# Another order of all steps, and batch 28 turned on VectorE, in a conditional adapter kernel

## The chip, the cores and the metric

One core of one Trainium2 chip. The engines are TensorE (PE in the profile, its weight loads PEld), VectorE (DVE), ScalarE (ACT), GpSimd (POOL) and SyncE (SP), which here only issues DMAs. The metric is the device time of one execution in microseconds; the median of several executions is given.

## The reference

For each of 128 batches, x is 128 x 512 in float32, and an index from 0 to 9 (cut to the range) picks the weights of one of ten languages. The batch goes down to 128 columns, through relu, up to 512 again, is added to x, normalized over its 512 columns, scaled and shifted, and added to x once more.

```python
w1 = W1[language_ids]
w2 = W2[language_ids]
h = jnp.einsum('bsh,bha->bsa', hidden_states, w1) + b1[language_ids][:, None, :]
h = jax.nn.relu(h)
adapted = jnp.einsum('bsa,bah->bsh', h, w2) + b2[language_ids][:, None, :]
x = hidden_states + adapted
mean = jnp.mean(x, axis=-1, keepdims=True)
var = jnp.mean(jnp.square(x - mean), axis=-1, keepdims=True)
normed = (x - mean) * jax.lax.rsqrt(var + LN_EPS)
return normed * gamma[language_ids][:, None, :] + beta[language_ids][:, None, :]
# and outside: x + that
```

## The kernel before

Every batch is one tile of 128 x 512. Its steps, with the engine of each, are: `transpose_x` (PE, four transposes into the one `pxT` buffer), `copy_xT` (ScalarE, to SBUF), `stage_w1` (a copy of the language's W1 into a `w1s` buffer, by ScalarE or, for batches of kind c, by GpSimd), `down` (PE, four matmuls into the one `ph` buffer), `relu` (ScalarE), `up` (PE, one matmul, shown as two, into one of five `py` buffers), `add_b2` (GpSimd, x + b2 into one of four `r` buffers), `residual` (VectorE, py + r with its row sum), `square` (ScalarE, with its row sum), then for a pair of batches `scalar_means` and `deviation` (ScalarE, the root) and three small steps `rstd` (VectorE), then `scale` (VectorE, by gamma), `add_beta` (GpSimd, x + beta into an output tile `o`, of which there are eight pairs) and `finish` (VectorE, which is the last to read `py`), and `store` of the pair (SyncE). x is loaded in pairs, x_g for batches 2g and 2g + 1, into eight buffers.

A string KINDS says where b2 comes in: P by `add_b2`, E by `seed` (ScalarE copies x into `py` first and `up` adds to it; `residual` then adds b2), D by an extra step `vector_b2` of VectorE, M by a small matmul. A string TURNS says how x is transposed and W1 arrives: T on PE with W1 staged by ScalarE, c the same with W1 staged by GpSimd, w with W1 loaded from memory, F "turned": W1 by four DMAs (`load_rows`), x by four more in blocks of 32 columns (`load_blocks`), and `turn_blocks`, one transpose on VectorE in place of four on PE and `copy_xT`.

The order is written out by hand. Each step has a place in batches in the table STEPS, its offset from its own batch: one tuple for the first 32 batches, one of 16 that repeats to batch 111, one for the last 16 batches. X_STEPS does the same for the loads of x from pair 10 on. All steps are sorted by batch + offset, and `keep` makes each engine run its own in that order. Of the last batches (E = 123) the steps stand in a written-out list, with `b2_of`, `beta_of`, `end_of`, `store_pair` and `store_last` for the same work. So a place decides nothing but the order on each engine's queue; each step still waits for its inputs and buffers. Each engine reads the language numbers of four batches at a time (`lid`).

Of the kernel before, what the change touches and what calls it, by code (L numbers as in the profile page):

```python
# [1008 lines left out]
```

## Time and profile before

| | |
|---|---|
| median of 3 runs | 301.0 us (300.9 to 301.27) |
| the profiled execution | 300.62 us, of which its span is 298.9 us |
| mean granted TensorE clock | 0.997 |
| busy: PE, DVE, ACT, POOL | 97%, 97%, 92%, 93% of the span |
| DMA | 85.22 MB, mean 285 GB/s |
| the chain that ended last | PE 75%, DMA 9%, POOL 6%, DVE 3% |

The span runs from the first to the last instruction of the profiled execution. In the profile L440 is `transpose_x`, L444 `copy_xT`, L431 `stage_w1`, L463 `down`, L471 `relu`, L477 and L485 `up`, L450 `add_b2`, L503 `residual`, L526 `square`, L569 `scale`, L457 `add_beta`, L578 `finish`, L663 `end_of`, L409 `turn_blocks`, L188 the load of an x pair, L397 and L403 the loads of a turned batch, L582 `store`, L695 and L698 the stores at the end. A line of waits gives the engine and line that waited, what it waited for, the total in us, how often, and the longest.

### The profile page before, as it was taken

To read this page: it belongs to the slowest core of one execution; us is meant where nothing else is said; L and a number is where in the kernel's file an instruction comes from. 1 tells how busy PE (TensorE), PEld (TensorE's weight loads), DVE (VectorE), ACT (ScalarE), POOL (GpSimd) and SP (SyncE) were. 2 spreads that over 40 slices of the span, in tenths; PEclk is the share of its full clock that TensorE was granted. 3 is DMA by queue.
4 is the path that set the end of the run, shared out by engine and by line. 5 is a ranking of instruction groups with operands and counts; after the bars stand their busy time and mean duration, and the time that the engine had idled before them with its cause. 6 is when DMAs were issued, how large, how long until landed. Compare 5 with 4: busy or idle time off the path is not lost.

```text
span 298.9 us, 7366 instructions
## 1 busy us (share of the span) xinstructions
PE 290.5 (97%) x1783; PEld 215.7 (72%) x1783; DVE 288.5 (97%) x775; ACT 274.4 (92%) x761; POOL 276.8 (93%) x239
## 2 busy tenths in 40 slices
PE   7899999999999999999999999999999999999993
PEld 3658777777776777767777777777777777777760
DVE  6989999999999999899999999999999999999996
ACT  5878789999999999989999999999999999899993
POOL 1299998999999999999899999999899999999992
PEclk9999999999999999999999999999999999999998
DMA  6999999955978798986999399986989879884907
GB/s 226 392 388 368 345 330 401 404 221 182 325 242 315 232 315 208 374 278 211 326 303 356 134 302 289 335 276 217 333 220 397 288 258 281 314 274 147 313 4 281
DMA packets 61100, 85.22 MB, mean 285 GB/s; under 512 B 4057, under 2 KB 25060, under 8 KB 61058
## 3 DMA queue, kind: packets, MB, share of 16 engines
q1 hardware_dynamic: 60998, 84.71, 84.1%
q8 instruction: 15, 0.25, 0.3%
q14 instruction: 27, 0.22, 0.2%
q10 hardware_dynamic: 60, 0.05, 0.1%
HBM read 51.19 MB, written 33.55 MB: 284 GB/s over the span
## 4 chain that ended last, share of the span: by engine, by line
PE 75%; DMA 9%; POOL 6%; DVE 3%; issue 3%; SPq 1%; POOLq 1%; ACT 1%; ACTq 0%; DVEq 0%
PE ph L463 30%; PE py L485 23%; PE pxT L440 14%; PE py L477 8%; POOL o L457 3%; DMA out_dram<-o 3%; DMA w<-in_L_cond_W_dram 3%; POOL r L450 2%; DMA x<-in_x_dram 2%; DVE py L503 1%; DVE o L663 1%; SPq L276 1%; POOLq L258 1%; DVE n L669 0%; DVE py L569 0%
## 5 line engine op out<-in xcount | busy, mean ns | idle before, releaser
L457 POOL TENSOR_TENSOR o<-x,beta_b 128x512 f32<-128x512 f32 x121 | 153.8, 1297 | 14.4 <-DVE beta_b L358 11.6
L463 PEld LDWEIGHTS ph<-xT,w1s 128*128 128x128 f32 x1024 | 126.8, 192 | 14.8 <-ACT hT L471 8.5
L463 PE MATMUL ph<-xT,w1s 128*128 128x128 f32 x1024 | 135.5, 275 | 0.3 <-DMA w1s<-in_L_cond_W_dram 0.2
L450 POOL TENSOR_TENSOR r<-x,b_b 128x512 f32<-128x512 f32 x83 | 107.1, 1299 | 1.6 <-DMA x<-in_x_dram 1.6
L485 PE MATMUL py<-w,hT 128*128 x196 | 101.1, 598 | 0.2 <-DMA w<-in_L_cond_W_dram 0.2
L440 PEld LDWEIGHTS pxT<-ident,x 128*128 128x128 f32 x468 | 59.9, 150 | 53.4 <-issue 39.9
L569 DVE SCALAR_TENSOR_TENSOR py<-py,nmean,gamma_b 128x512 f32<-128x512 f32 x124 | 93.1, 752 | 0.0
L578 DVE SCALAR_TENSOR_TENSOR o<-py,rstd,o 128x512 f32<-128x512 f32 x116 | 85.7, 746 | 2.7 <-DVE py L569 1.6
L526 ACT ACTIVATE sq<-py,sum 128x512 f32<-128x512 f32 x124 | 85.5, 690 | 0.4 <-DVE rstd L545 0.3
L444 ACT COPY xT<-pxT 128x512 f32<-128x512 f32 x117 | 68.6, 586 | 5.6 <-PE pxT L440 5.5
L440 PE MATMUL pxT<-ident,x 128*128 128x128 f32 x468 | 71.2, 275 | 1.3 <-ACT gamma_b L343 0.7
L503 DVE SCALAR_TENSOR_TENSOR py<-py,r 128x512 f32<-128x512 f32 x88 | 60.8, 691 | 0.7 <-PE py L485 0.5
L471 ACT ACTIVATE hT<-ph,b1T 128x128 f32<-128x128 f32 x128 | 47.3, 369 | 8.2 <-PE ph L463 5.9
L431 ACT COPY w1s<-w 128x512 f32 x80 | 48.6, 618 | 1.2 <-issue 1.2
L485 PEld LDWEIGHTS py<-w,hT 128*128 128x128 f32 x196 | 29.9, 192 | 2.4 <-DMA w<-in_L_cond_W_dram 0.7
L477 PE MATMUL py<-w,hT 128*128 x60 | 30.7, 594 | 0.0
L526 ACT ACTIVATION_READ_ACCUMULATOR sq<-py,sum 128x1 f32 x124 | 25.5, 205 | 0.0
L503 DVE SCALAR_TENSOR_TENSOR py<-py,b_b 128x512 f32<-128x512 f32 x30 | 20.6, 688 | 0.0
L423 ACT COPY py<-x 128x512 f32<-128x512 f32 x30 | 17.9, 598 | 0.2 <-DVE o L578 0.2
L536 ACT ACTIVATE root<-ssq,eps 128x2 f32<-128x2 f32 x62 | 16.8, 271 | 0.4
L517 ACT ACTIVATE nmean<-sum 128x2 f32<-128x2 f32 x61 | 12.6, 207 | 0.5 <-DVE py L503 0.2
L503 DVE DVE_READ_ACCUMULATOR py<-py,r 128x1 f32 x88 | 12.3, 140 | 0.0
(80 smaller groups left out, 149.4 us busy)
## 6 DMA issues: line engine op xcount, KB each, us to landing
x<-in_x_dram SPq DMA_DIRECT2D x64, 512.0 KB, 5.6
out_dram<-o SPq DMA_DIRECT2D x62, 512.0 KB, 4.5
w1s<-in_L_cond_W_dram SPq DMA_DIRECT2D x25, 256.0 KB, 7.4
w1s<-in_L_cond_W_dram SPq DMA_DIRECT2D x44, 64.0 KB, 4.9
x<-in_x_dram SPq DMA_DIRECT2D x44, 64.0 KB, 2.3
w<-in_L_cond_W_dram SPq DMA_DIRECT2D x4, 640.0 KB, 8.1
w<-in_L_cond_W_dram SPq DMA_DIRECT2D x1, 1792.0 KB, 9.8
w<-in_L_cond_W_dram SPq DMA_DIRECT2D x1, 768.0 KB, 5.3
```

The source lines that it names most:

```text
L431: keep(nc.gpsimd.tensor_copy(dst, src) if gpsimd else nc.scalar.copy(dst, src))
L440: keep(nc.tensor.transpose(pxs[b][:, k, :], cols, ident))
L444: keep(nc.scalar.copy(xT[b], pxs.pop(b)))
L450: keep(nc.gpsimd.tensor_tensor(rs[b], xb(b), b2_b[:, bass.ds(v * H, H)], ALU.add))
L457: keep(nc.gpsimd.tensor_tensor(os[g][:, j, :], xb(b), beta_b[:, bass.ds(v * H, H)], ALU.add))
L463: nc.tensor.matmul(phs[b], lhsT=w1s[b][:, k, :], rhs=xT_of(b, k), start=(k == 0), stop=(k == KC - 1))
L477: keep(nc.tensor.matmul(ys[b], lhsT=hT[b], rhs=cols, start=False, stop=True, skip_group_check=True))
L485: keep(nc.tensor.matmul(ys[b], lhsT=hT[b], rhs=w2[:, bass.ds(v * H, H)], start=not m, stop=True))
L503: nc.vector.scalar_tensor_tensor(ys[b], ys[b], 1.0, r, ALU.mult, ALU.add, accum_out=sum_of(b))
L526: nc.scalar.activation(sq, ys[b], AF.Square, bias=col(sums, b), scale=-float(H), accum_out=col(ssqs, b))
L569: nc.vector.scalar_tensor_tensor(ys[b], ys[b], col(nmeans, b), gamma_b[:, bass.ds(v * H, H)], ALU.add, ALU.mult)
L578: nc.vector.scalar_tensor_tensor(o, ys[b], rstds[g][:, j : j + 1], o, ALU.mult, ALU.add)
```

## The change

Batch 28 becomes a turned batch. Of the last 16 batches, 113 and 119 have W1 staged by ScalarE, 120 by GpSimd. Nearly all places in STEPS and X_STEPS change, those of the first 32 batches too, which had been the same from batch to batch; `up` of 2 and 3 come before `transpose_x` of 5. The loads of turned batches and of x and the stores stand at other places of SyncE's queue. The list of the end is in another order, with the stores of its pairs earlier in it. KINDS stays, and the work of every step stays as it was. The diff is cut to the tables that the text below speaks of and to both ends of the list.

```diff
@@ -22,122 +22,122 @@
-TURNS = ('TTTTTTTTTTTTTTTTTTTTTTTTTTTTTTTT', 'TTcTFTTTTTwTFTTT', 'ccccFcTcTcTTTTTT')
+TURNS = ('TTTTTTTTTTTTTTTTTTTTTTTTTTTTFTTT', 'TTcTFTTTTTwTFTTT', 'cTccFcTTccTTTTTT')
     "load": (
-        (0, 0, 0, 0, 0, 0, 0, 0, 0, 0, 0, 0, 0, 0, 0, 0, 0, 0, 0, 0, 0, 0, 0, 0, 0, 0, 0, 0, 0, 0, 0, 0,),
-        (0, 0, 0, 0, -4, 0, 0, 0, 0, 0, -2.81, 0, -3.51, 0, 0, 0,),
-        (0, 0, 0, 0, -6.42, 0, 0, 0, 0, 0, 0, 0, 0, 0, 0, 0,),
+        (0, 0, 0, 0, 0, 0, 0, 0, 0, 0, 0, 0, 0, 0, 0, 0, 0, 0, 0, 0, 0, 0, 0, 0, 0, 0, 0, 0, -0.68, 0, 0, 0,),
+        (0, 0, 0, 0, -4.44, 0, 0, 0, 0, 0, -0.85, 0, -5.67, 0, 0, 0,),
+        (0, 0, 0, 0, -1.63, 0, 0, 0, 0, 0, 0, 0, 0, 0, 0, 0,),
     "transpose": (
-        (0, 0, 0, 0, 0, 0, 0, 0, 0, 0, 0, 0, 0, 0, 0, 0, 0, 0, 0, 0, 0, 0, 0, 0, 0, 0, 0, 0, 0, 0, 0, 0,),
-        (-0.22, -0.2, -0.19, 0.29, 0, -1.03, -1.53, -0.9, -0.44, -0.96, -0.24, -0.56, 0, -1.37, -0.58, 0.02,),
-        (-0.56, -0.3, -0.31, -0.45, 0, -0.93, -0.02, -0.27, 0.56, 0.88, 0, 0, 0, 0, 0, 0,),
+        (-0.31, -0.37, -0.12, -0.15, -0.15, -1.1, -0.11, -0.19, -0.52, -0.01, -0.49, 0.07, -0.5, 0.09, -0.31, -0.17, 0.49, 0.48, 0.27, 0.16, -0.08, -0.14, -0.25, -0.24, -0.01, 0.08, -0.1, -0.4, 0, -1.6, -0.4, -0.11,),
+        (-0.55, -0.47, -0.47, -0.56, 0, -0.94, -0.75, -0.2, -0.56, -1.01, -0.6, -0.78, 0, -1.38, -0.09, -0.64,),
+        (-0.48, -0.29, -0.45, -0.66, 0, -1.11, -0.43, -0.17, 0.75, 1.66, 0, 0, 0, 0, 0, 0,),
     "turn": (
-        (0, 0, 0, 0, 0, 0, 0, 0, 0, 0, 0, 0, 0, 0, 0, 0, 0, 0, 0, 0, 0, 0, 0, 0, 0, 0, 0, 0, 0, 0, 0, 0,),
-        (0, 0, 0, 0, 0.2, 0, 0, 0, 0, 0, 0, 0, -0.57, 0, 0, 0,),
-        (0, 0, 0, 0, -0.45, 0, 0, 0, 0, 0, 0, 0, 0, 0, 0, 0,),
+        (0, 0, 0, 0, 0, 0, 0, 0, 0, 0, 0, 0, 0, 0, 0, 0, 0, 0, 0, 0, 0, 0, 0, 0, 0, 0, 0, 0, 0.09, 0, 0, 0,),
+        (0, 0, 0, 0, -0.49, 0, 0, 0, 0, 0, 0, 0, -0.22, 0, 0, 0,),
+        (0, 0, 0, 0, -0.31, 0, 0, 0, 0, 0, 0, 0, 0, 0, 0, 0,),
...
     "down": (
-        (1.1, 1.1, 1.1, 1.1, 1.1, 1.1, 1.1, 1.1, 1.1, 1.1, 1.1, 1.1, 1.1, 1.1, 1.1, 1.1, 1.1, 1.1, 1.1, 1.1, 1.1, 1.1, 1.1, 1.1, 1.1, 1.1, 1.1, 1.1, 1.1, 1.1, 1.1, 1.1,),
-        (1.07, 1.07, 1.42, 0.73, 0.41, 0.34, 0.33, 0.77, 0.9, 0.77, 0.77, 0.62, 0.63, 0.68, 1.17, 1.04,),
-        (1.28, 0.93, 0.89, 0.87, 1.38, 1.13, 1.04, 1.62, 3.44, 0, 0, 0, 0, 0, 0, 0,),
+        (0.58, 0.79, 1.2, 0.88, 1.31, 1.41, 1.09, 1.08, 1.09, 0.71, 1.29, 1.51, 1.26, 1.38, 1.03, 1.49, 1.6, 1.43, 1.17, 1.29, 1.22, 1.24, 1.21, 1.05, 1.34, 1.13, 0.85, 0.4, 1.03, 0.77, 0.96, 0.59,),
+        (1.04, 1.14, 0.56, 0.68, 0.15, 0.49, 0.89, 0.46, 0.06, 0.61, 1.09, 0.54, 1.06, 1.06, 0.9, 0.62,),
+        (1.27, 0.86, 0.57, 0.99, 1.01, 0.87, 2.29, 1.92, 3.7, 0, 0, 0, 0, 0, 0, 0,),
...
     "beta": (
-        (1.06, 1.06, 1.06, 1.06, 1.06, 1.06, 1.06, 1.06, 1.06, 1.06, 1.06, 1.06, 1.06, 1.06, 1.06, 1.06, 1.06, 1.06, 1.06, 1.06, 1.06, 1.06, 1.06, 1.06, 1.06, 1.06, -0.13, -0.13, -0.13, -0.13, -0.13, -0.13,),
-        (-1.6, 2.27, 3.38, 2.95, -2.25, -1, -1.17, 1.07, 3.14, 1.65, 4.45, 0.87, 4.05, -0.07, 3.92, 4.77,),
-        (-0.44, -0.9, 2.33, 3.63, 7.85, 8.64, 1.39, 1.88, 5.26, 0, 0, 0, 0, 0, 0, 0,),
+        (2.03, 2.01, 2.58, 2.49, 0.89, -1.02, 3.47, -0.14, 1.3, 0.42, 0.71, -0.16, -1.59, 5.06, 0.69, 3.45, 5.63, 3.93, 1.82, 4.4, 1.71, 3, 5.36, 2.46, 1.64, 2.84, -0.2, 3.34, 2.23, 1.46, 0.1, 4.86,),
+        (0.07, 3.23, 5.05, 2.81, 0.16, -2.13, 3.04, -1.64, 4.08, 4.47, 4.97, 1.01, 6.29, -1.87, 3.56, 4.55,),
+        (-1.83, 5.97, 4.7, 5.01, 5.92, 11.06, 1.95, -1.25, 4.58, 0, 0, 0, 0, 0, 0, 0,),
     "seed": (
-        (0, 0, 0, 0, 0, 0, 0, 0, 0, 0, 0, 0, 0, 0, 0, 0, 0, 0, 0, 0, 0, 0, 0, 0, 0, 0, 0, 0, 1.69, 0, 0, 0,),
-        (1.8, 0, 0, 0, 0, 0, 1.37, 0, 1.91, 0, 1.58, 0, 2.14, 0, 0, 0,),
-        (1.5, 0, 1.96, 0, 2.03, 0, 0, 0, 7.66, 0, 0, 0, 0, 0, 0, 0,),
+        (0, 0, 0, 0, 0, 0, 0, 0, 0, 0, 0, 0, 0, 0, 0, 0, 0, 0, 0, 0, 0, 0, 0, 0, 0, 0, 0, 0, 1.94, 0, 0, 0,),
+        (1.83, 0, 0, 0, 0, 0, 1.64, 0, 1.87, 0, 1.57, 0, 1.83, 0, 0, 0,),
+        (1.6, 0, 1.85, 0, 1.74, 0, 0, 0, 8.35, 0, 0, 0, 0, 0, 0, 0,),
     "up": (
-        (2.5, 2.5, 2.5, 2.5, 2.5, 2.5, 2.5, 2.5, 2.5, 2.5, 2.5, 2.5, 2.5, 2.5, 2.5, 2.5, 2.5, 2.5, 2.5, 2.5, 2.5, 2.5, 2.5, 2.5, 2.5, 2.5, 2.66, 2.66, 2.66, 2.66, 2.66, 2.66,),
-        (2.44, 2.68, 2.08, 2.03, 2.03, 1.39, 2, 2.68, 2.19, 2.18, 2.2, 2.11, 2.48, 2.43, 2.57, 2.35,),
-        (2.34, 2.49, 2.18, 2.48, 2.67, 2.21, 3.39, 8.45, 0, 0, 0, 0, 0, 0, 0, 0,),
+        (2.23, 2.32, 0.5, 0.32, 2.51, 2.23, 2.46, 2.37, 2.58, 2.39, 2.87, 2.33, 2.52, 2.22, 3.07, 2.75, 2.59, 2.31, 2.64, 2.54, 2.68, 2.47, 2.19, 2.87, 2.5, 2.11, 2.41, 2.74, 2.27, 1.97, 1.68, 2.12,),
+        (2.16, 2.67, 2.08, 1.36, 1.79, 2.32, 1.91, 1.84, 2.1, 2.52, 2.1, 2.22, 2.26, 2.18, 1.9, 2.37,),
+        (2.22, 2.73, 2.72, 2.49, 1.93, 3.53, 3.92, 7.16, 0, 0, 0, 0, 0, 0, 0, 0,),
...
     "end": (
-        (6.66, 6.66, 6.66, 6.66, 6.66, 6.66, 6.66, 6.66, 6.66, 6.66, 6.66, 6.66, 6.66, 6.66, 6.66, 6.66, 6.66, 6.66, 6.66, 6.66, 6.66, 6.66, 6.66, 6.66, 6.66, 6.66, 6.67, 6.32, 6.67, 6.32, 6.67, 6.32,),
-        (5.98, 6.29, 6.75, 6.24, 6.44, 5.78, 6.53, 5.87, 7.65, 5.95, 7.26, 6.26, 6.91, 5.9, 6.65, 6.26,),
-        (7.86, 5.73, 9.72, 6.91, 0, 0, 0, 0, 0, 0, 0, 0, 0, 0, 0, 0,),
+        (6.31, 6.65, 6.96, 6.06, 6.85, 6.13, 6.97, 6.48, 7.18, 6.64, 6.64, 5.73, 7.18, 6.43, 7.16, 7.14, 7.42, 6.54, 7.08, 6.13, 6.88, 6.08, 6.89, 6.16, 6.9, 6.28, 6.72, 5.91, 7.06, 5.82, 6.11, 5.89,),
+        (6.82, 5.96, 5.94, 5.67, 6.79, 5.89, 6.81, 5.89, 7.41, 5.67, 6.97, 5.97, 7.03, 5.94, 6.1, 5.9,),
+        (8.16, 6.74, 11.18, 10.03, 0, 0, 0, 0, 0, 0, 0, 0, 0, 0, 0, 0,),
     "store": (
-        (7.66, 0, 7.66, 0, 7.66, 0, 7.66, 0, 7.66, 0, 7.66, 0, 7.66, 0, 7.66, 0, 7.66, 0, 7.66, 0, 7.66, 0, 7.66, 0, 7.66, 0, 7.32, 0, 7.32, 0, 7.32, 0,),
-        (11.86, 0, 8.21, 0, 11.29, 0, 12.28, 0, 8.34, 0, 13.61, 0, 10.64, 0, 11.08, 0,),
-        (11.18, 0, 11.79, 0, 0, 0, 0, 0, 0, 0, 0, 0, 0, 0, 0, 0,),
+        (10.11, 0, 11.75, 0, 14.05, 0, 10.61, 0, 8.65, 0, 11.99, 0, 10.88, 0, 9.42, 0, 11.37, 0, 19.06, 0, 8.72, 0, 8.93, 0, 15.76, 0, 9.39, 0, 11.81, 0, 11.79, 0,),
+        (13.54, 0, 11.42, 0, 9.48, 0, 14.04, 0, 13.22, 0, 13.77, 0, 13.1, 0, 12.96, 0,),
+        (21.53, 0, 16.97, 0, 0, 0, 0, 0, 0, 0, 0, 0, 0, 0, 0, 0,),
-X_STEPS = (-9.01, -11.0, -7.01, -9.0, -7.01, -9.0, -3.85, -2.46, -7.41, -3.42, -4.57, -8.85, -6.51, -1.91, -3.85, -2.46, -7.41, -3.42, -4.57, -8.85, -6.51, -1.91, -3.85, -2.46, -7.41, -3.42, -4.57, -8.85, -6.51, -1.91, -3.85, -2.46, -7.41, -3.42, -4.57, -8.85, -6.51, -1.91, -3.85, -2.46, -7.41, -3.42, -4.57, -8.85, -6.51, -1.91, -8.46, -7.54, -6.99, -6.46, -0.43, -6.98, -7.95, 0.41)
+X_STEPS = (-6.26, -5.92, -3.79, -7.8, -2.61, -6.17, -4.41, -8.47, -7.67, -2.65, -1.74, -6.92, -7.54, -1.88, -4.41, -8.47, -7.67, -2.65, -1.74, -6.92, -7.54, -1.88, -4.41, -8.47, -7.67, -2.65, -1.74, -6.92, -7.54, -1.88, -4.41, -8.47, -7.67, -2.65, -1.74, -6.92, -7.54, -1.88, -4.41, -8.47, -7.67, -2.65, -1.74, -6.92, -7.54, -1.88, -6.81, -8.77, -6.16, -4.04, -1.4, -3.28, -7.08, -4.24)
@@ -823,151 +823,151 @@
     lid(E + 1, ET.PE)
     lid(E + 1, ET.SP)
     transpose_x(E - 1)
+    copy_xT(E - 1)
     rstd(E // 2 - 3, 2)
-    copy_xT(E - 1)
-    beta_of(E)
-    b2_of(E - 2)
     down(E - 2)
-    up(E - 3)
-    beta_of(E - 2)
+    relu(E - 2)
     residual(E - 4)
-    relu(E - 2)
-    square(E - 4)
     rstd(E // 2 - 3, 3)
     scale(E - 6)
+    b2_of(E + 2)
+    square(E - 4)
+    b2_of(E - 2)
+    deviation(E // 2 - 2)
+    up(E - 3)
+    scalar_means(E // 2 - 2)
     end_of(E - 7)
     residual(E - 3)
-    deviation(E // 2 - 2)
+    rstd(E // 2 - 2, 1)
+    end_of(E - 6)
+    rstd(E // 2 - 2, 2)
     transpose_x(E)
...
+    diag_of(E + 2, nc.scalar)
     scale_out(E + 2)
-    square_of(E + 4)
+    base_of(E + 2, p_y, "y")
+    root_of(E + 4)
+    mean_of(E + 4, nc.scalar)
     rstd_of(E + 3, 1)
-    diag_of(E + 2, nc.scalar)
+    base_of(E + 4, p_y, "y")
     rstd_of(E + 3, 2)
-    gamma_of(E + 1)
-    add_of(E + 1, halves[1])
+    add_of(E + 1, halves[0])
     rstd_of(E + 3, 3)
-    root_of(E + 4)
-    base_of(E + 4, p_y, "y")
+    product_of(E + 2)
+    store_last(E + 1, nc.sync, halves[1])
     scale(E + 3)
-    store_pair(E // 2 - 2)
     rstd_of(E + 4, 1)
+    store_last(E + 1, nc.sync, halves[0])
     end_of(E + 3)
-    add_of(E + 1, halves[0])
-    store_pair(E // 2 - 1)
     rstd_of(E + 4, 2)
-    mean_of(E + 4, nc.scalar)
-    product_of(E + 2)
     rstd_of(E + 4, 3)
-    store_pair(E // 2)
     copy_out(E + 2)
     scale_out(E + 4)
+    store_last(E + 3, nc.sync)
     end_of(E + 4, halves[1])
-    store_last(E + 1, nc.sync, halves[1])
-    store_last(E + 1, nc.sync, halves[0])
-    store_last(E + 3, nc.sync)
     store_last(E + 2, nc.sync)
+    store_last(E + 4, nc.sync, halves[1])
     end_of(E + 4, halves[0])
-    store_last(E + 4, nc.sync, halves[1])
     store_last(E + 4, nc.sync, halves[0])
```

More of the change, by code (lines that the diff above doesn't have):

```diff
@@ L825, in cond_resid_kernel @@
     transpose_x(E - 1)
+    copy_xT(E - 1)
     rstd(E // 2 - 3, 2)
-    copy_xT(E - 1)
-    beta_of(E)
-    b2_of(E - 2)
     down(E - 2)
-    up(E - 3)
-    beta_of(E - 2)
+    relu(E - 2)
     residual(E - 4)
-    relu(E - 2)
-    square(E - 4)
     rstd(E // 2 - 3, 3)
     scale(E - 6)
+    b2_of(E + 2)
[4 more added lines that the diff above has]
+    scalar_means(E // 2 - 2)
     end_of(E - 7)
     residual(E - 3)
-    deviation(E // 2 - 2)
+    rstd(E // 2 - 2, 1)
+    end_of(E - 6)
+    rstd(E // 2 - 2, 2)
     transpose_x(E)
-    rstd(E // 2 - 2, 1)
+    copy_xT(E)
     down(E - 1)
-    scalar_means(E // 2 - 2)
-    copy_xT(E)
     up(E - 2)
     stage_w1(E)
-    end_of(E - 6)
+    relu(E - 1)
+    stage_w1(E + 1)
     b2_of(E - 1)
-    rstd(E // 2 - 2, 2)
     scale(E - 4)
-    relu(E - 1)
+    square(E - 3)
     transpose_x(E + 1)
+    down(E)
+    copy_xT(E + 1)
+    beta_of(E - 2)
     b2_of(E)
-    b2_of(E + 2)
+    beta_of(E)
+    up(E - 1)
     rstd(E // 2 - 2, 3)
-    stage_w1(E + 1)
-    down(E)
     scale(E - 5)
-    square(E - 3)
+    transpose_x(E + 2)
+    relu(E)
+    down(E + 1)
     residual(E - 2)
-    copy_xT(E + 1)
-    up(E - 1)
-    end_of(E - 4)
-    relu(E)
-    beta_of(E - 1)
-    square(E - 2)
-    deviation(E // 2 - 1)
-    transpose_x(E + 2)
-    down(E + 1)
-    scalar_means(E // 2 - 1)
+    scalar_means(E // 2 - 1)
+    load_late(E + 2)
+    b2_of(E + 1)
+    square(E - 2)
+    end_of(E - 5)
+    deviation(E // 2 - 1)
+    end_of(E - 4)
+    load_late(E + 3)
     copy_xT(E + 2)
-    end_of(E - 5)
+    beta_of(E + 3)
     residual(E - 1)
     up(E)
+    load_late(E + 4)
     relu(E + 1)
-    transpose_x(E + 3)
     rstd(E // 2 - 1, 1)
-    load_late(E + 2)
-    down(E + 2)
-    square(E - 1)
-    copy_xT(E + 3)
     rstd(E // 2 - 1, 2)
     scale(E - 2)
+    square(E - 1)
+    transpose_x(E + 3)
     rstd(E // 2 - 1, 3)
+    down(E + 2)
+    copy_xT(E + 3)
     residual(E)
+    end_of(E - 2)
     square(E)
     relu(E + 2)
-    end_of(E - 2)
-    b2_of(E + 1)
     deviation(E // 2)
     negative_means(E // 2)
-    beta_of(E + 1)
     up(E + 1)
@@ L896, in cond_resid_kernel @@
     transpose_x(E + 4)
+    n_of(E - 3, False)
     scale(E - 1)
-    load_late(E + 3)
     down(E + 3)
-    n_of(E - 3, False)
-    beta_of(E + 3)
     copy_xT(E + 4)
@@ L904, in cond_resid_kernel @@
     rstd(E // 2, 1)
+    beta_of(E - 1)
     residual(E + 1)
+    gamma_of(E - 3)
     rstd(E // 2, 2)
     mean_of(E + 1, nc.vector)
+    up(E + 2)
     relu(E + 3)
```

39 lines of the change are left out of this document (21 added, 18 removed), and 74 rows, old and new, of the table STEPS.

## The prediction

> **What bounds the kernel now.** I read the page first: busy shares, then the stretches of 20 us, then the chain that ended last, then the waits engine by engine.
>
> ```profile
> span 298.9 us, 7366 instructions
> PE 290.5 (97%) x1783; PEld 215.7 (72%) x1783; DVE 288.5 (97%) x775; ACT 274.4 (92%) x761; POOL 276.8 (93%) x239
> 20.00:30.00 10.00, 10.00 (x67) 7.89 (x66) 9.90 (x26) 8.71 (x27) 10.00 (x9) 1.00 1.07 371
> 30.00:40.00 10.00, 10.00 (x63) 7.63 (x62) 9.78 (x26) 7.93 (x23) 10.00 (x9) 1.00 1.12 336
> 40.00:60.00 20.00, 20.00 (x130) 15.37 (x129) 19.92 (x53) 18.23 (x52) 19.01 (x17) 1.00 1.07 388
> 60.00:80.00 20.00, 20.00 (x131) 15.26 (x129) 19.85 (x53) 19.88 (x58) 20.00 (x17) 1.00 0.65 233
> ```
>
> The columns of a stretch are its length, then the busy time of PE, PEld, DVE, ACT and POOL, the clock, the DMA share and GB/s. TensorE (PE) and VectorE (DVE) are both full, GpSimd (POOL) nearly, and the clock is granted in full. So four engines run in balance, and an order of steps can only win what they lose by waiting on one another. How much that is, I read from PE's starts.
>
> ```profile
> 94.14 0.86 PE py L485 x2
> 95.44 0.89 PE ph L463 x8
> 96.33 0.86 PE py L485 x2
> 107.28 0.86 PE py L477 x2
> 108.14 0.89 PE ph L463 x8
> 109.03 0.86 PE py L485 x2
> 17.34 1.02 PE L485 MATMUL py<-w,hT 128*128 x2
> 289.50 0.38 PE L484 MATMUL py<-parts,pick 96*128 96x512 bf16 x1
> 289.72 1.02 PE L485 MATMUL py<-w,hT 128*128 x2
> ```
>
> The first six lines are from the chain, the last three from the timeline of PE. A batch whose x is transposed on PE takes 96.33 - 94.14 = 2.19 us; one that VectorE turns takes 109.03 - 107.28 = 1.75 us, so the four transposes cost 0.44 us. `up` of batch 1 starts at 17.34 and `up` of batch 127, the last, at 289.72: 272.4 us. Between them lie 113 batches at 2.19 (247.5), 11 turned ones at 1.75 (19.3), two `up`s more than `down`s (1.7) and two bias matmuls of 289.72 - 289.50 = 0.22 (0.4): 268.9. About 3.5 us (1.3%) is all that PE loses, from the first `up` to the last. That is the ceiling of what another order can win there, beside work taken off PE.
>
> By the Trainium skill, Perfetto Trace Analysis, section Identifying the Most-Contended Engine, PE's room is judged by LDWEIGHTS (here 72%) and not by matmul busy time (97%); by that PE would have much room and VectorE would be the bound. The starts above, back to back, speak against it; what follows if it is right is the slower rival below.
>
> **The change, part by part.** *Batch 28 turned.* It was transposed by PE, copied by ScalarE and given a staged W1.
>
> ```profile
> L444 ACT COPY xT<-pxT 128x512 f32<-128x512 f32 x117 | 68.6, 586 | 5.6 <-PE pxT L440 5.5
> L431 ACT COPY w1s<-w 128x512 f32 x80 | 48.6, 618 | 1.2 <-issue 1.2
> 123.82 0.71 DVE L409 STREAM_TRANSPOSE xT<-x 128x512 f32<-128x512 f32 x1
> 124.45 0.12 DVE L545 SCALAR_TENSOR_TENSOR rstd<-part,root 128x2 f32<-128x2 f32 x1
> x<-in_x_dram SPq DMA_DIRECT2D x44, 64.0 KB, 2.3
> w1s<-in_L_cond_W_dram SPq DMA_DIRECT2D x44, 64.0 KB, 4.9
> ```
>
> PE loses 0.44 us of work, on the path: -0.44. ScalarE loses a copy of 0.59 us and gains room; the W1 copies stay 80 (28's goes; of the last 16 batches 113 and 119 move from GpSimd to ScalarE, 120 the other way), so GpSimd loses one copy and ScalarE has none more. VectorE gets one transpose; the next instruction follows 124.45 - 123.82 = 0.63 us after it, so +0.63 there. What hides it: VectorE must have 0.63 us idle near batch 28, which is up at about 77 us. In the four stretches quoted it idles 0.10 + 0.22 + 0.08 + 0.15 = 0.55 us. The cover is thin; it is helped by PE's results for the later batches coming 0.44 us sooner. I put it at nothing on the path, and at +0.63 if the cover is gone. SyncE's queue gets eight DMAs of 64 KB more. By the list they stand only 28.09 - 27.32 = 0.77 batches (1.7 us) before the turn, less than the 2.3 us to landing; but the queue runs ahead of the list. What stands before them is the load of x_17, which waits until `add_beta` of batch 19 (23.4 by the list) has read x_9: four batches, some 9 us, ahead of the turn. At nothing, with a bound of 4.9 us less the 1.71 batches (3.7 us) to `down`: +1.2. The DMA share in 60:80 is 0.65, so 0.5 MB finds room.
>
> *Loads and stores at other places of SyncE's queue.* This queue is served in order, and a store that waits for VectorE holds up the loads behind it.
>
> ```profile
> 83.93 0.43 SPq L188 DMA_DIRECT2D x<-in_x_dram  x1
> 84.47 0.41 SPq L582 DMA_DIRECT2D out_dram<-o  x1
> 84.97 6.65 DMA x<-in_x_dram
> 91.76 0.63 PE L440 MATMUL pxT<-ident,x 128*128 128x128 f32 x4 [0.42 <-DMA x<-in_x_dram]
> POOL o L457 <- DMA x<-in_x_dram: 1.8, 3, 0.8
> POOL r L450 <- DMA x<-in_x_dram: 1.6, 2, 1.3
> POOL o L457 <- DMA out_dram<-o: 1.0, 1, 1.0
> ```
>
> The load at 84.97 is x_19 (batches 38 and 39). It stands behind the store of batches 26 and 27, issued 0.5 us earlier, lands at 91.62, and PE's transposes of batch 38 wait 0.42 us for it: the largest single wait of PE past the start. By the lists: the load used to be free to go at batch 33.6 (`finish` of 27 stands at 33.3 and takes 0.3) and has its first transposes at 36.5, 2.9 batches later; now it stands ahead of that store and can go at 30.9 (when `add_beta` of 27, at 30.3 and 0.6 long, has freed x_13 for the load in front of it), with the transposes at 37.2, 6.3 batches. The least such lead of all loads of the middle rises from 2.4 batches to 4.6 (about 10 us against 6.65 to landing). So this wait goes, -0.42, and so should most of GpSimd's 1.8 + 1.6 us. Stores move to 9 to 19 batches after theirs (before: 8 to 14); what they free is an output tile of eight pairs, and GpSimd's one wait for it (1.0 us) should not come back, since `add_beta` mostly runs later as well. GpSimd's gain lies beside PE's path: nothing.
>
> *The start.* `up` of 2 and 3 go ahead of the transposes of 5.
>
> ```profile
> 18.20 0.63 PE L440 MATMUL pxT<-ident,x 128*128 128x128 f32 x4
> 18.67 1.02 PE L485 MATMUL py<-w,hT 128*128 x2
> 19.56 0.75 PE L440 MATMUL pxT<-ident,x 128*128 128x128 f32 x4
> 20.15 1.06 PE L463 MATMUL ph<-xT,w1s 128*128 128x128 f32 x8
> 21.04 1.02 PE L485 MATMUL py<-w,hT 128*128 x2
> 22.51 1.06 PE L463 MATMUL ph<-xT,w1s 128*128 128x128 f32 x8
> 23.60 0.37 ACT L471 ACTIVATE hT<-ph,b1T 128x128 f32<-128x128 f32 x1 [0.31 <-PE ph L463]
> ```
>
> From `up` of 2 (18.67) to `down` of 5 (22.51) are 3.84 us. Two `up`s, two sets of transposes at 18.67 - 18.20 = 0.47 and one `down` make 3.55, so PE lost 0.3 us here. In the new order only the transposes of 6 (0.47 us) lie between `down` of 4 and `down` of 5, and `relu` of 4 (the 0.37 us of the last row is one such) has to end between them, since there is one `ph` buffer: 0.37 and a hand-over of at most the 0.31 that ScalarE waited there, less 0.47, loses up to 0.2 again. The work is the same: zero, from -0.3 to +0.2.
>
> *All other steps reordered.* The trace of before can't show what waits the new order has.
>
> ```profile
> 126.56 0.30 PEld L485 LDWEIGHTS py<-w,hT 128*128 128x128 f32 x2 [0.24 <-DVE o L578]
> 134.55 0.63 PEld L463 LDWEIGHTS ph<-xT,w1s 128*128 128x128 f32 x5 [0.30 <-ACT hT L471]
> PEld ph L463 <- ACT hT L471: 8.5, 26, 0.5
> ```
>
> One wait of this kind costs 0.24 to 0.30 us at the weight load, and not all of it at the matmul. Of the 3.5 us lost, 0.42 was x_19 0.3 lies at the start, and 0.4 is no wait (the transposes of batches 4 to 16 take 0.47 and not 0.44), so some 2.4 us is order. Bounds: all of it goes (-2.4), or as much comes again (+2.4). In the steady list the two closest pairs of `end` and the step that takes over its `py` buffer were 0.08 and 0.09 batches apart; the closest is now 0.25. In the first 32 batches it is the reverse: five of 26 are closer than 0.25 batches, and were one. I take -0.15.
>
> *The tail.* The last steps of VectorE, PE and ScalarE keep their order. Stores of batches 120 to 123 can go a little sooner, but the last store waits for the last `end_of`. Zero.
>
> Sum: -0.44 - 0.42 - 0.15 = -1.0 us. Against the profiled execution, 300.62 us (span 298.9 and 1.7 around it), that is 299.6; the median shown is 301.0, 0.4 higher, so I forecast 300.0. A measurement of this kernel can tell 0.2%, 0.6 us, from no change.
>
> **The rivals.** *Most waits go.* -0.44 - 0.42 and 2.1 of the 2.4, so 298.0 (chance 0.12). For it: ScalarE has 8% idle to give. Against: DVE at 97% leaves little play.
>
> *New waits for old.* The new order loses at other places about the 0.9 us that x_19 and batch 28 save: 301.0 (0.18). For it: 26 waits on `hT` are a matter of chance in any list.
>
> *VectorE takes over, slower.* Batch 28's turn takes the 0.55 us that VectorE had idle, `end` then comes later for every batch behind it, and PE's `up` waits for its `py` buffer. Price: +0.63, and five close pairs at 0.24 (1.2), -0.44 for PE: +1.4, so 302.4 (0.28). It decides if VectorE has less than 0.63 us to spare in 20 to 80 us; the row of 60:80, 19.85 of 20, speaks for it, PE's whole 20.00 there against it. The page's rule on LDWEIGHTS, named above, would lead here.
>
> *Not what it says.* Order in the code is order on each engine, so a list that comes to the same order would give 300.6 to 301.0; the places in the diff differ too much for that, and I leave it inside the second rival.
>
> **How the numbers follow.** Forecast 0.42, most waits go 0.12, new for old 0.18, VectorE 0.28. Faster by over 0.2% takes the first two and a little of the third's spread, 0.56; within 0.2% is most of the third and a rim of the others, 0.16; slower is VectorE's, 0.28. The forecast's own range is 299.3 to 300.7. For 8 in 10 the range goes from 298.4 (most of the first rival outside) to 302.4, VectorE's price.
>
> **What would show it.** Right: the profile after has no wait of PE's transposes on a DMA of x near 90 us; POOL's waits on x fall below 1 us; `up` of 1 to `up` of 127 takes 271.4 us; one transpose more at L409, four PE transposes fewer. Wrong: PE's busy share in 60:100 falls, with waits of L485's weight loads on DVE's L578 of well over 0.6 us in total; or a wait of PE's `down` of 28 on a DMA, the late load.

## The result, and the profile after

The change takes 303.22 us (median; 301.32 to 305.64). The kernel before, run beside it on the same chip, takes 300.63 us (300.11 to 301.27). The ratio is 1.0088, with a 95% interval of 1.0062 to 1.0113: 0.9% slower, where 300.0 us and a gain were forecast. The spread is wider as well, 4.3 us where the kernel before has 1.2 here and 1.9 to 2.6 in the groups of runs further down. The profiled execution after took 302.32 us.

The page after, its first lines, which answer to those that the prediction quotes of before:

```profile
span 300.6 us, 7343 instructions
PE 292.3 (97%) x1779; PEld 216.3 (72%) x1779; DVE 288.8 (96%) x776; ACT 273.3 (91%) x760; POOL 276.4 (92%) x238
```

The stretches of the span after, with the columns that the prediction explains:

```profile
20.00:30.00 10.00, 9.76 (x65) 7.89 (x64) 9.75 (x25) 8.39 (x27) 10.00 (x9) 1.00 1.07 371
40.00:60.00 20.00, 20.00 (x127) 15.20 (x126) 19.90 (x54) 18.10 (x51) 19.25 (x17) 1.00 1.03 374
60.00:80.00 20.00, 20.00 (x127) 15.17 (x126) 20.00 (x53) 19.19 (x56) 20.00 (x17) 1.00 0.84 262
80.00:100.00 20.00, 19.92 (x128) 15.00 (x127) 19.82 (x53) 19.44 (x54) 20.00 (x18) 1.00 0.78 261
100.00:120.00 20.00, 19.82 (x124) 14.45 (x123) 19.07 (x52) 19.31 (x56) 19.64 (x17) 1.00 0.91 299
120.00:140.00 20.00, 19.39 (x121) 14.32 (x120) 19.44 (x51) 18.20 (x54) 20.00 (x18) 1.00 0.89 306
```

The same stretches of the kernel before, where the prediction did not look:

```profile
80.00:100.00 20.00, 19.58 (x126) 14.82 (x125) 19.48 (x51) 19.31 (x55) 20.00 (x18) 1.00 0.83 272
100.00:120.00 20.00, 20.00 (x130) 15.35 (x129) 19.90 (x55) 19.72 (x56) 19.36 (x17) 1.00 0.85 256
120.00:140.00 20.00, 19.94 (x123) 14.69 (x123) 19.06 (x49) 18.93 (x54) 20.00 (x17) 1.00 0.82 291
```

But for 0.24 us between 20 and 30 us PE is full to 80 us in both, around batch 28 too, and between 80 and 100 us it is fuller than before (19.92 against 19.58). From 100 to 140 us it loses 0.73 us more than before. So most of what PE loses up to the last `up` is lost neither at the start nor at batch 28.

What the prediction named as signs came as it said. The timeline of PE after, around batch 28 (start, duration, operation):

```profile
74.68 1.02 PE L485 MATMUL py<-w,hT 128*128 x2
75.54 1.05 PE L463 MATMUL ph<-xT,w1s 128*128 128x128 f32 x8
76.43 1.12 PE L477 MATMUL py<-w,hT 128*128 x2
```

The timeline of SyncE's queue after, around the load of x_19:

```profile
81.09 0.90 SPq L188 DMA_DIRECT2D x<-in_x_dram  x2
83.86 0.38 SPq L582 DMA_DIRECT2D out_dram<-o  x1
```

From `up` of 27 to `up` of 28 are 1.75 us and no transposes. x_19, the second of the two loads at 81.09, goes ahead of the store of batches 26 and 27, and in the whole list of waits after no engine waits for a DMA of x any more. Yet from `up` of 1 to `up` of 127 the change takes 273.5 us, not 271.4; the timeline of PE has these two:

```profile
17.42 1.02 PE L485 MATMUL py<-w,hT 128*128 x2
290.88 1.02 PE L485 MATMUL py<-w,hT 128*128 x2
```

Of the 1.7 us by which the profiled execution is longer, 1.1 lie between these two. Another 0.5 lie behind the last `up`: from there to the end of the span it is 9.7 us, before 9.1.

**Where the new loss is.** The largest stall of PE after is this one. First the timeline of ScalarE, then that of PE; the bracket gives the idle time before the instruction, and what ended it.

```profile
133.93 0.39 ACT L471 ACTIVATE hT<-ph,b1T 128x128 f32<-128x128 f32 x1
135.67 0.69 ACT L526 ACTIVATE sq<-py,sum 128x512 f32<-128x512 f32 x1 [1.35 <-DVE o L578]
```

```profile
135.67 1.02 PE L485 MATMUL py<-w,hT 128*128 x2
137.31 0.66 PE L440 MATMUL pxT<-ident,x 128*128 128x128 f32 x4 [0.61 <-ACT xT L444]
```

The view of one source line shows what lies in between: L258 is `lid`, each engine's reads of language numbers, with their count, shortest/median/longest in ns, and the start of the first and last.

```profile
L258 ACTq TENSOR_LOAD <-lang x1: 1847/1847/1847, 133.7 to 133.7; - x1
```

ScalarE idles 1.35 us, and PE's transposes then wait 0.61 us for its copy. The profile names VectorE's L578 as what ended the idle time. But the read that stands ahead of `square` in ScalarE's queue ran from 133.7 to 135.55, and `square` starts 0.1 us later. A read is no busy time of the engine. While it runs, the engine's sequencer hands out nothing behind it; the engine finishes what it was given before (here some 0.5 us of work) and then stands. The median read takes 0.32 us and mostly hides behind that work. This one took 1.85.

By the Trainium skill, Perfetto Trace Analysis, section Sequencer-only Instruction, the sequencer turns to the next instruction only when such an instruction has been executed and its semaphore update pushed. The trace agrees: 1.35 us idle behind 1.85 us of read. The Trainium skill, DMA: Bandwidth & Descriptors, section Latency and other measured facts, gives such a load a floor of about 600 ns; here four numbers take 0.29 to 0.34 us at the least, so the measurement decides.

VectorE shows the same after, in the view of L258 and its own timeline. ScalarE then waits 0.43 us for a result of VectorE (its L517 at 103.52), and PE's weight loads, in the last two lines, wait for `relu`. That both of these waits come from this one read is not shown, since ScalarE has a slow read of its own at 106.9 (0.92 us).

```profile
L258 DVEq TENSOR_LOAD <-lang x1: 1704/1704/1704, 100.8 to 100.8; - x1
```

```profile
102.62 0.16 DVE L542 SCALAR_TENSOR_TENSOR part<-part,root 128x2 f32<-128x2 f32 x1 [0.83 <-DVE py L569]
```

```profile
106.16 0.97 PEld L463 LDWEIGHTS ph<-xT,w1s 128*128 128x128 f32 x8 [0.93 <-ACT hT L471]
108.35 0.97 PEld L463 LDWEIGHTS ph<-xT,w1s 128*128 128x128 f32 x8 [0.56 <-ACT hT L471]
```

The kernel before has such reads too, here in its view of L258, with VectorE's timeline behind the first:

```profile
L258 DVEq TENSOR_LOAD <-lang x1: 1834/1834/1834, 119.1 to 119.1; - x1
L258 ACTq TENSOR_LOAD <-lang x1: 901/901/901, 132.3 to 132.3; - x1
```

```profile
121.08 1.41 DVE L578 SCALAR_TENSOR_TENSOR o<-py,rstd,o 128x512 f32<-128x512 f32 x2 [0.84 <-DVE py L569]
```

These two reads stand ahead of the very two waits, at 126.56 and 134.55, from which the prediction priced "order". The third row of that place in the prediction, 26 waits on `hT` of 8.5 us in all, is no measure of what PE loses: in the run of the kernel before without the reads, further down, 26 such waits remain, and PE then loses 0.8 us in all between `up` of 1 and `up` of 127:

```profile
PEld ph L463 <- ACT hT L471: 8.3, 26, 0.4
```

All 32 reads of either engine, in the same view of the kernel before and then of the change:

```profile
L258 ACTq TENSOR_LOAD <-lang x32: 304/310/948, 8.0 to 268.6; - x32
L258 DVEq TENSOR_LOAD <-lang x32: 340/344/1834, 18.5 to 273.7; - x32
```

```profile
L258 ACTq TENSOR_LOAD <-lang x32: 304/319/1847, 9.8 to 268.8; - x32
L258 DVEq TENSOR_LOAD <-lang x32: 341/346/2003, 18.6 to 275.0; - x32
```

### The profile page after: what moved, and what is told of

It is laid out like the page before. It is cut to its first block, busy times and chain, and to the rows that moved or that the text cites. A ratio compares the mean times of both kernels' runs of the same rounds, so it can differ in the third digit from the quotient of the medians.

```text
span 300.6 us, 7343 instructions
## 1 busy us (share of the span) xinstructions
PE 292.3 (97%) x1779; PEld 216.3 (72%) x1779; DVE 288.8 (96%) x776; ACT 273.3 (91%) x760; POOL 276.4 (92%) x238
## 5 line engine op out<-in xcount | busy, mean ns | idle before, releaser
L457 POOL TENSOR_TENSOR o<-x,beta_b 128x512 f32<-128x512 f32 x121 | 152.0, 1281 | 12.7 <-DVE beta_b L358 12.7
L450 POOL TENSOR_TENSOR r<-x,b_b 128x512 f32<-128x512 f32 x83 | 105.1, 1277 | 3.4 <-POOL w1s L431 2.6
L485 PE MATMUL py<-w,hT 128*128 x196 | 100.7, 596 | 0.1
L526 ACT ACTIVATE sq<-py,sum 128x512 f32<-128x512 f32 x124 | 86.6, 698 | 5.3 <-DVE py L503 1.4
L578 DVE SCALAR_TENSOR_TENSOR o<-py,rstd,o 128x512 f32<-128x512 f32 x116 | 85.1, 748 | 2.4 <-DVE py L569 1.2
L471 ACT ACTIVATE hT<-ph,b1T 128x128 f32<-128x128 f32 x128 | 48.1, 376 | 4.3 <-PE ph L463 2.0
L485 PEld LDWEIGHTS py<-w,hT 128*128 128x128 f32 x196 | 30.1, 192 | 1.9 <-issue 1.1
L526 ACT ACTIVATION_READ_ACCUMULATOR sq<-py,sum 128x1 f32 x124 | 26.3, 212 | 0.0
L517 ACT ACTIVATE nmean<-sum 128x2 f32<-128x2 f32 x61 | 13.1, 214 | 0.9 <-DVE rstd L545 0.4
```

The lines of the kernel that those rows point to most:

```text
L450: keep(nc.gpsimd.tensor_tensor(rs[b], xb(b), b2_b[:, bass.ds(v * H, H)], ALU.add))
L457: keep(nc.gpsimd.tensor_tensor(os[g][:, j, :], xb(b), beta_b[:, bass.ds(v * H, H)], ALU.add))
L471: keep(nc.scalar.activation(hT[b], phs.pop(b), AF.Relu, bias=b1T[:, bass.ds(lid(b, ET.Activation), 1)]))
L485: keep(nc.tensor.matmul(ys[b], lhsT=hT[b], rhs=w2[:, bass.ds(v * H, H)], start=not m, stop=True))
L526: nc.scalar.activation(sq, ys[b], AF.Square, bias=col(sums, b), scale=-float(H), accum_out=col(ssqs, b))
L578: nc.vector.scalar_tensor_tensor(o, ys[b], rstds[g][:, j : j + 1], o, ALU.mult, ALU.add)
```

## The experiments

All runs were timed beside the kernel before on the same chip; its median was 300.22 to 300.84 us in the seven groups, and each ratio is to that.

**The queue.** The change with the old places of stores and x loads, and the reverse.

```diff
# after_old_queue: the change, with before's
-    "store", X_STEPS of the change
+    "store", X_STEPS of before (no store ahead of its last finish)
# before_new_queue: the kernel before, with the change's
-    "store", X_STEPS of before
+    "store", X_STEPS of the change
```

> The changed kernel with the places of stores and x loads in SyncE's queue put back to those of before (a store no earlier than its last finish allows; batch 28 stays turned, with its loads where the change has them). Theory A, the queue: the new places bunch loads and stores, register loads of language numbers that fall into such a bunch take 0.9 to 2.0 us in place of 0.3, and engines stall behind them; then this gives 300.0 to 300.8 us with a spread under 1 us, and fewer than 45 register loads over 0.5 us (61 after, 40 before). Theory B, the order of the compute steps: 302.5 to 303.5 us with a spread of 3 us, as the change. Theory C, VectorE lacks room for the turn of batch 28: the same as B.

> The kernel before with only the store places and x load places of the change. Theory A (queue): 301.5 to 303 us, a wider spread than the 1 us of before, and over 50 register loads above 0.5 us. Theory B (order of the compute steps) and theory C (turn of batch 28): 300.2 to 301.0, since the wait of batch 38 on its x load goes (-0.4).

Measured: 303.66 us (ratio 1.0107, 1.0072 to 1.0143) and 299.83 us (0.9970, 0.9953 to 0.9987). The new places alone cause no loss; in the old order of the other steps they gain 0.85 us, twice the 0.42 that the prediction gave x_19. Theory A fails in both runs, though the slow reads came as it said: 56 reads took over 0.5 us in `before_new_queue` and 46 in `after_old_queue` (40 in the kernel before, 61 in the change). On ScalarE and VectorE, the engines that turn out to matter below, the old order with the new places has 21 such reads, as many as the change, and is faster than before all the same. The first run is muddied: with the old places the turn of batch 28 waits for its own blocks, which cost about 1.2 us at that point (its timeline of VectorE):

```profile
73.01 0.71 DVE L409 STREAM_TRANSPOSE xT<-x 128x512 f32<-128x512 f32 x1 [1.28 <-DMA x<-in_x_dram]
```

**Twice the numbers in a read.**

```diff
-G = 4
+G = 8
```

> The changed kernel with language numbers read for eight batches at a time (half as many register loads on each engine, at the places of every second one). If slow register loads, whatever makes them slow, are what holds PE up: about half of what they cost goes, 300.8 to 302.0 us, and the spread shrinks. If it is waits between the steps themselves: within 0.3 us of 303.2.

> The kernel before, with the language numbers read for 8 batches at a time and not for 4, as in the run of the change with that (300.10 us, 3.1 less than the change). Theory L (slow reads of language numbers cost the new order time that the old order covers): the old order gains at most 0.6 us, 300.0 to 300.7 us. Theory M (such reads cost any order alike, and the new order loses by its own waits): it gains about the 3 us that the change gained, 297.5 to 298.5 us.

Measured: the change 300.10 us (0.9980, 0.9963 to 0.9997), below the 300.8 that was the least expected, the kernel before 303.43 us (1.0101, 1.0074 to 1.0128). Both theories of the second run fell: half as many reads took 3.1 us off one order and put 3.2 us on the other. In the slowed kernel the stalls are again behind reads, now longer ones. The largest, in the view of L258 and the timelines of VectorE and PE of `before_lid8`:

```profile
L258 DVEq TENSOR_LOAD <-lang x16: 593/600/2344, 18.8 to 268.7; - x16
```

```profile
128.56 0.70 DVE L503 SCALAR_TENSOR_TENSOR py<-py,r 128x512 f32<-128x512 f32 x1 [1.30 <-POOL o L457]
```

```profile
130.04 1.12 PE L485 MATMUL py<-w,hT 128*128 x2 [0.91 <-DVE o L578]
```

So the number of reads alone does not decide. That it is which of them is slow, and what the engine has left to do meanwhile, fits these rows but is not shown by them.

**Batch 28 alone, and parts of the list.**

```diff
# before_turn28: the kernel before, with
-TURNS = ('TTTTTTTTTTTTTTTTTTTTTTTTTTTTTTTT', ...
+TURNS = ('TTTTTTTTTTTTTTTTTTTTTTTTTTTTFTTT', ...
+    "load" of 28: -3.51, "turn" of 28: -0.57
# old_first32: the change, with the first tuples of STEPS and TURNS, and the first six of X_STEPS, of before
# new_first32: the kernel before, with the same parts of the change
# new_steady: the kernel before, with the second tuples, and X_STEPS of batches 32 to 111, of the change
```

> The kernel before with only batch 28 turned, its loads 3.51 batches and its turn 0.57 batches ahead of it as the later turned batches have. Theories A and B: -0.44 us for PE's four transposes, 300.0 to 300.4. Theory C (VectorE lacks the 0.63 us): 300.8 to 301.8.

> The change, with the places of the first 32 batches as before (batch 28 on TensorE too); the steady part, the end and the stores and loads that belong to them stay changed. Theory F (the first 32 batches and the turn of 28 on VectorE carry the loss): 300.4 us or less. Theory S (the steady order and the end carry it): it loses the 0.4 us of batch 28 again and stays at 303.0 us or more.

> The kernel before, with the changed places of the first 32 batches alone, batch 28 turned. Theory F (this part carries the loss): 302.5 us or more. Theory S (the steady order and the end carry it): 300.3 us, the 0.44 us of batch 28 gained and nothing lost; x_19 still waits, since its load keeps its old place.

> The kernel before, with the changed places of the repeating part alone (batches 32 to 111). Theory S1 (the steady order carries the loss, where slow reads of language numbers find it): 302.0 us or more, with a spread of 3 us. Theory S2 (the end carries it): 300.6 us or less, since x_19's wait of 0.42 us goes too.

Measured: 302.47 us (1.0053, 1.0030 to 1.0077), 309.37 (1.0285, 1.0244 to 1.0327), 301.77 (1.0045, 1.0020 to 1.0070) and 309.35 (1.0306, 1.0274 to 1.0339). The two of 309 us say nothing of the parts: both join the old first 32 batches to the new steady list, and at that seam an x load goes too late; both lose 4.6 us within batches 36 to 39. A row of PE's timeline in `new_steady`:

```profile
101.30 0.63 PE L440 MATMUL pxT<-ident,x 128*128 128x128 f32 x4 [2.77 <-DMA x<-in_x_dram]
```

`new_first32` lies between its two theories, and loses 1.3 us at its own seam (batch 31). `before_turn28` put the turn too early, so that VectorE waits there, and PE for VectorE (timelines of both, `before_turn28`):

```profile
70.44 0.71 DVE L409 STREAM_TRANSPOSE xT<-x 128x512 f32<-128x512 f32 x1 [0.88 <-ACT xT L444]
```

```profile
73.19 1.13 PE L485 MATMUL py<-w,hT 128*128 x2 [1.09 <-DVE part L542]
```

In the change the turn starts at 71.64 and has waited for nothing. The gain of the turn is thus a matter of its place: VectorE has no 0.9 us to spare there, as the rival said.

**Without the reads.** The test that settled it.

```diff
     def lid(b, engine):
-        g = b // G
+        g = min(b // G, 1)
```

> The change, with the language numbers read for the first 8 batches only; every later batch uses the number of batch b % 4 + 4, so the outputs of batches 8 to 127 use other languages' weights, while every step, transfer and place stays. It leaves out 30 of the 32 reads of each engine. Theory L (slow reads of language numbers cost the new order time, and it would else gain): at most as long as the kernel before without reads, and 0.4 to 1.0 us shorter if the terms -0.44 and -0.42 hold; that is 298 us or less. Theory M (waits of the new order's own): 302 us or more, and 2 us or more above the kernel before without reads.

> The kernel before, with the language numbers read for the first 8 batches only (later batches use the number of batch b % 4 + 4). Theory L: its traced reads over 0.5 us cost PE about 1.5 us, so 299.0 to 299.6 us, and the change without reads is shorter than this. Theory M: 300.5 us, the reads cost it nothing.

Measured: the change 298.53 us (298.27 to 298.68; 0.9919, 0.9894 to 0.9944), the kernel before 298.77 us (298.50 to 298.93; 0.9930, 0.9905 to 0.9954). Each spreads over 0.4 us. Theory L holds in its main part, though the old order came out below its 299.0 to 299.6: the reads cost the new order 303.22 - 298.53 = 4.7 us and the old one 300.77 - 298.77 = 2.0, and the difference, 2.7 us, is the loss of the change (2.6). The spread of the times is the reads' too. What failed is the gain expected without them, 0.4 to 1.0 us: it is 0.24. From `up` of 1 to `up` of 127 both take nearly the same, 269.7 (before) and 269.9 us; batch 28 gives its 0.4, and waits of the new order's own in the first 32 batches take 0.6 back. The largest of these, near batch 31, in the timeline of PE's weight loads of `after_no_reads`:

```profile
82.48 0.97 PEld L463 LDWEIGHTS ph<-xT,w1s 128*128 128x128 f32 x8 [0.31 <-ACT hT L471]
```

**Which engines.** Reads left out by engine, in the change.

```diff
-        g = b // G
+        g = min(b // G, 1) if engine in (ET.Activation, ET.DVE) else b // G    # after_reads_rest
+        g = b // G if engine in (ET.Activation, ET.DVE) else min(b // G, 1)    # after_reads_act_dve
```

> The change; ScalarE and VectorE read language numbers for the first 8 batches only (later batches use the number of batch b % 4 + 4 in their steps), TensorE, GpSimd and SyncE read all as in the change. Theory L1 (the reads of the two engines that feed TensorE carry the 4.7 us): 298.5 to 299.7 us. Theory L2 (the reads of TensorE itself, GpSimd and SyncE carry it): 302 us or more.

> The change; TensorE, GpSimd and SyncE read language numbers for the first 8 batches only, ScalarE and VectorE read all as in the change. Theory L1: 302 us or more, with a spread of 2 us or more. Theory L2: 298.5 to 299.7 us. If the cost adds up by engine, this run and the other one lie together 4.7 us above twice 298.5 us.

Measured: 299.19 us (0.9948, 0.9929 to 0.9968) and 303.84 us (1.0097, 1.0073 to 1.0122). Theory L1: ScalarE's and VectorE's reads carry the loss, the 87 reads of the other three engines some 0.7 us. The costs do not add up by engine (0.7 + 5.3 is more than 4.7): with the other reads gone, 12 of ScalarE's 32 took over 0.8 us, against 8 in the change; why is open.

**Fewer reads, with every number still read.** Four numbers of 4 bits in one value, packed once; a shift and a mask at each use.

```diff
+    packed = l0 + 16 * l1 + 256 * l2 + 4096 * l3, by VectorE (packed) or by GpSimd (late_pack)
-                lang[0:1, g * G : (g + 1) * G],
+                packed[0:1, g * 4 : (g + 1) * 4],   # 16 batches; late_pack: from batch 16 on
-        return lids[g, engine][b % G]
+        return (lids[g, engine][b % 16 // 4] >> (4 * (b % 4))) & 15
```

> The change, with four language numbers packed into one value at the start (six small VectorE steps), so that a read of four values serves 16 batches: 8 reads for each engine instead of 32, and a shift and a mask of a register at each use. Theory L (the loss goes with the number of reads that fall among loads and stores of 512 KB): the 4.7 us that the reads cost the change shrink to a quarter, 298.5 + 1.2 = 299.7 us (299.2 to 300.3). Theory Q (what a read costs is the work of the engines' sequencers, and arithmetic on registers costs as much): 302 us or more.

> The kernel before, with the same packing. Theory L: the 2.0 us that the reads cost it shrink to a quarter, 298.8 + 0.5 = 299.3 us (298.9 to 299.8). Theory Q: 301 us or more.

> The kernel before, with four language numbers packed into one value, but the first 16 batches read as before and the packing done by GpSimd while it has nothing else to do at the start: 11 reads for each engine instead of 32. The 2.8 us that the packing on VectorE cost at the start should go: theory L gives 298.8 us plus 11/32 of 2.0 us and 0.3 us for shifts and masks, 299.8 us (299.2 to 300.3). If shifts and masks on full engines cost more than the reads they save, 300.7 us or more.

> The kernel before, with both: the stores and loads of x at their changed places and the late packing on GpSimd. If the two gains add up (0.85 us for the places), 299.0 us (298.5 to 299.6), below every kernel so far that computes the reference. If fewer reads leave the places nothing to gain, 299.8 us as the run beside it.

Measured: `after_packed` 302.25 us (1.0050, 1.0032 to 1.0069), `before_packed` 301.53 (1.0036, 1.0016 to 1.0055), `before_late_pack` 303.05 (1.0080, 1.0057 to 1.0103), `queue_late_pack` 299.96 (0.9978, 0.9963 to 0.9993). All four gains that were expected of fewer reads failed to come, and the times are those of the rivals (of theory Q in the first two). The traces show only part of why. Packing on VectorE put off the first `up` by 2.3 us in `before_packed` and 1.6 in `after_packed`. From `up` of 1 to `up` of 127 the packing won time in these two, 2.4 us in the new order (271.0 us after 273.5) and 1.0 in the old (271.4 after 272.4), and 0.5 to 0.6 us went behind the last `up`. `before_late_pack` has no such delay and is slower still; its trace from the first `up` to the last is within 0.3 us of the kernel before, 1.2 us more lie behind the last, and I have no shown cause. `queue_late_pack` is no better than `before_new_queue`. The shifts and masks make some 1,280 instructions more, on engines that are full; the page of `before_packed` begins:

```profile
span 300.7 us, 8647 instructions
```

**The places of the reads.** The packets' records of the DMA engines show when a 512 KB load or store of 2 KB rows is under way. In the eight traces with all reads of four numbers at their old places (the two kernels, the two runs of the queue and the four of batch 28 and the list), from 40 us on, of 231 reads that began with none under way 6% took over 0.5 us; of 776 that began beside one, 45%. (The expectation below has an earlier count.) In the old order the gaps between these transfers lie, counted by `up`, at about batches 5 to 7.75, with one store inside in most, and 13.25 to 14.5 of each 16; ScalarE and VectorE each have one of their four reads in the first gap (at 5.7 and 6.9). In the change that gap is at about 2.25 to 4.5, and the reads stayed (at 6.1 and 7.1). One such read of VectorE took 343 ns before and 1,704 after. The view of L258 and the stretch of 2 us around it, before (last column GB/s):

```profile
L258 DVEq TENSOR_LOAD <-lang x1: 343/343/343, 100.3 to 100.3; - x1
```

```profile
99.00:101.00 2.00, 2.00 (x15) 1.54 (x14) 2.00 (x6) 1.92 (x7) 2.00 (x3) 1.00 0.47 114
```

The stretches after:

```profile
99.00:101.00 2.00, 2.00 (x15) 1.65 (x14) 1.96 (x5) 1.61 (x6) 2.00 (x3) 1.00 1.01 253
101.00:103.00 2.00, 2.00 (x15) 1.66 (x14) 1.17 (x5) 2.00 (x6) 2.00 (x2) 1.00 0.76 194
```

So reads alone were moved, into the gaps:

```diff
+MOVED = {
+    ET.Activation: {20: 13.6, 24: 13.9, 28: 14.2, 32: 26.9, 36: 32.3, ...},
+    ET.DVE: {20: 13.6, 24: 13.9, 28: 26.8, 32: 32.2, 36: 32.4, ...},
+}
...
-                if on(n):
+                if on(n) and n // G * G not in MOVED.get(engine, {}):
                     at(b + 0.99, lid, n, engine)
...
+    for engine, places in MOVED.items():
+        for n, place in places.items():
+            at(place, lid, n, engine)
```

> The change, and only the places of ScalarE's and VectorE's reads of language numbers moved: 26 of ScalarE's 32 and 25 of VectorE's are read earlier, at places where the trace of the change shows no load or store of 512 KB under way (around batches 11, 24, 30, 36, 45, 50 to 52, 60, 66 to 68, 77, 82 to 84, 92, 98 to 100 and 110). No read is taken away, and the queue and all other steps keep their order. Over eight traces 2% of the reads in such gaps took over 0.5 us, and 40 to 52% of those among the transfers. Theory L (the loss is where the reads of these two engines fall among those transfers): most of the 4.0 us that leaving these reads out won comes back, 299.3 to 300.5 us, below the change by 2.5 us or more, with under 10 reads over 0.5 us on the two engines together (21 in the change). Theory N (the number of reads counts, not their places): 302.5 us or more.

> The kernel before with the changed places of stores and loads of x (299.83 us alone), and the reads of language numbers of ScalarE, VectorE and TensorE moved into the gaps that its own trace shows between the transfers of 512 KB (around batches 11, 26, 30, 37, 45, 50 to 53, 60, 66 to 69, 76, 82 to 85, 92, 98 to 102, 108 and 118): 26, 25 and 26 of the 32 of each. Theory L: between 299.83 and the 298.77 us of the kernel before without reads, 299.2 us (298.8 to 299.6), faster than every kernel so far that computes the reference. Theory N (number, not place): 299.8 us.

Measured: `after_quiet_reads` 300.67 us (0.9991, 0.9968 to 1.0013), which is 2.55 us below the change with the same number of reads, and 0.2 above the range of theory L. On the two engines 6 reads took over 0.5 us, against 21, and the longest are shorter (the same view; `lid` is L262 here):

```profile
L262 ACTq TENSOR_LOAD <-lang x32: 303/308/930, 9.8 to 266.6; - x32
L262 DVEq TENSOR_LOAD <-lang x32: 340/343/794, 18.7 to 272.5; - x32
```

The place of the reads counts, not their number alone: theory N is out. That the reads became shorter (6 slow ones, not 21) is the likely reason; what the engines have left to do at the new places changed too, and no run parts the two. The run stays 1.5 us above the kernel without these reads, and still spreads over 3.1 us; behind two pairs of short moved reads ScalarE idles 0.44 and 0.45 us, and behind three single ones some 0.2, but that this is all of it is not shown. `queue_quiet_reads` took 299.67 us (0.9963, 0.9947 to 0.9980), the best ratio of all kernels that read every number, though not to be told from `before_new_queue` (0.9970). This missed theory L's 298.8 to 299.6 and is nearer to theory N's 299.8: 8 slow reads on ScalarE and VectorE in place of 21 won nothing clear in the old order of the other steps. So the moved places pay in the new order, and a slow read has no fixed price. Both runs are faster than the two kernels of this case.

## Why the prediction was wrong

*Batch 28, -0.44.* Held: 1.75 us in place of 2.19, at the place forecast. VectorE covered the turn (PE 20.00 of 20 in 60:80). The late blocks, bound +1.2, did not come here, but did with the old queue (1.28 us).

*x_19, -0.42, and GpSimd's waits.* Held: the waits are gone, and the queue's places alone gain 0.85 us. Without reads the old order has no such wait either, so it was a near miss that a little delay turned into a wait.

*Start and tail.* The start lost 0.24 us more of PE in 20:30 than forecast (0). The tail was forecast at zero too and took 0.5 us more in the profiled execution; without reads it took 0.3 less than before (9.2 against 9.5 us).

*All other steps, -0.15 within ±2.4.* This step failed. It took the 2.4 us that PE lost, beyond x_19 and the start, as waits that the order of steps makes and another order may lose. But 272.4 us from `up` of 1 to `up` of 127 become 269.7 without reads: 2.6 of the 3.5 us lost went with the reads, x_19's 0.42 among them, and both rows that were to show the price of order, 126.56 and 134.55, follow a slow read on the engine that they name. Without the reads both are gone: `up` follows `up` there after 2.19 us, and after 1.75 for the turned batch, where the kernel before took 2.35 and 2.51 (batches 50 and 54) and 1.99 (51). The term should have been how much the new order pays for reads. In the profiled executions that is 273.46 - 269.93 = 3.5 us against 272.38 - 269.74 = 2.6 before; by the medians, 4.7 against 2.0. Those 2.7 us turn the rest, a gain of 0.24, into a loss of about 2.5 (measured: 2.6).

*The moved stores and loads.* They were weighed by who waits for them. That they also decide which reads fall beside a transfer was not seen. The run with the quiet reads shows that in the new order most of the loss goes when the reads of two engines are moved. It does not show that the moved stores and loads brought the loss: with them alone the old order gained 0.85 us, and with the old places the new order still took 303.66 us. Why the new order of the other steps pays more for slow reads than the old one stays open.

*The rival "VectorE takes over".* It named the side, and 302.4 us is near, but not the mechanism: its signs did not come. PE's busy share fell after 100 us, not in 60:100 (39.92 of 40 us after, 39.58 before), and L485's weight loads wait 0.5 us in total for L578, not well over 0.6. That four engines run without slack is why a late read of two of them can cost PE time; this fits the rows, but no run isolates it. Its doubt about the cover was sound: `before_turn28` shows it. As for the rule on LDWEIGHTS named there (the Trainium skill, Perfetto Trace Analysis, Identifying the Most-Contended Engine): without reads the kernel before needs 269.7 us where PE's own work sums to 268.9, with LDWEIGHTS at 73%, so PE was the bound and the trace does not agree with the rule here.
